# Turning the rows and columns of a segment softmax by block transposes on VectorE, and spreading destination scores by a transfer

## The chip, the cores and the metric

The kernel runs on one core of a Trainium2 chip. The metric is the device time of one execution in microseconds (us). The core has five engines that each work through an instruction queue of their own in order: TensorE (PE in the profile, PEld for its weight loads), VectorE (DVE), ScalarE (ACT), GpSimd (POOL) and SyncE (SP, which only issues transfers here). They meet through semaphores. SBUF is the on-chip memory of 128 partitions, PSUM the smaller memory that TensorE writes its products into.

## What is computed

A graph attention layer over 12,500 nodes of 64 features and 400,000 edges of 64 features, the edges sorted by destination. In the reference, without its helpers:

```python
h_src = nfeats[src]
h_dst = nfeats[dst]
z_att = jnp.concatenate([h_src, h_dst, efeats], axis=-1)
e = jax.nn.leaky_relu(z_att @ W_attn + b_attn, negative_slope=0.01)[:, 0]
m = jnp.concatenate([h_src, efeats], axis=-1) @ W_ne
emax = jax.ops.segment_max(e, dst, num_segments=N)
ex = jnp.exp(e - emax[dst])
denom = jax.ops.segment_sum(ex, dst, num_segments=N)
alpha = ex / denom[dst]
z = jax.ops.segment_sum(alpha[:, None] * m, dst, num_segments=N)
out = jax.nn.relu(jnp.concatenate([nfeats, z], axis=-1) @ W_out)
```

The result is the layer norm of x + out over the features.

## The kernel before

**Tiling.** A group is 512 edges: 128 partitions (p) of 4 consecutive edges (t). There are 782 groups. The first 83 full ones, whose few destinations have very many edges each, are the dense part (the generator `dense_part`, three chunks of 32, 28 and 24 groups). The others are cut into 36 chunks of 20 groups (the last two are shorter), and a chunk into parts of SG = 4 groups, 175 parts in all. The edges of one group have destinations inside a window of S = 48 nodes, so a one-hot of 48 columns against a group's first destination says where an edge goes.

**A chunk.** The loop over chunks does this, in program order:
- `indices` and `slots_of` turn the source and destination numbers of a chunk two ahead into columns (TensorE transposes L155, ScalarE copies).
- For each part, `gather` loads the edge features ze by one SyncE transfer (L181) and the source rows zx by 16 indirect transfers that GpSimd issues (L190). Both come from rings of ZB = 8 buffers. Then `scores` computes the attention scores. It loads wrow, 48 destination scores for each of the 4 groups, as one row on one partition (L202); a TensorE matmul of that row with ones_row (L203) copies it to all 128 partitions, into win. VectorE then runs a chain: L207 (ze times the attention weights w_edge), L209 (sum), L214, L216 (the one-hot, hot), L221 (hot times win), L224 (sum), L225, L226 (leaky relu), about 5.8 us a part. The tile fixed is one PSUM bank that holds slots, w_edge, w_src, alpha and win.
- `softmax` works on the whole chunk. The scores are block transposed (L294), so that a partition holds a row of 128 consecutive edges: partition h*32+g has the h-th quarter of group g. Segments run across the rows, so each of the four running maxima and sums goes in three steps: a scan in each row (L298, L313, L329 and others), a scan over the row results in one line on one partition (L305, L317, L340), and a second scan in each row that starts from the value carried in (L308, L321, L342). `to_row` brings a column of 128 results to one line in the order of the edges: a TensorE matmul with the permuted identity order (L232), read from PSUM. `to_col` brings the line back to a column: VectorE permutes it (L237), TensorE multiplies it by a 1x1 one (L240), VectorE copies the column from PSUM (L242). A softmax has four of each. Three more rows, rw, say where a segment runs on from row to row (L284 to L286 on VectorE, L289 on TensorE, L291 on ScalarE), and fac1, one number that rescales the node shared with the chunk before, is spread to a column in the same manner (L357, L359). ScalarE copies the scores in edge order (e, L296), takes the exponentials (L328, L338) and copies the result to alpha in PSUM (L350).
- `aggregate`, for each part: VectorE makes w = hot times alpha (L365), TensorE 32 float32 matmuls of 64x48 (L373) into a PSUM tile pg, and VectorE adds the four groups of it to acc, the accumulator of all nodes, at an offset read from a register (L383).

A step of `dense_part` is called after each part's scores and after every second part's aggregation, and `finish` writes an output block (layer norm and so on) as soon as its nodes are complete. The dense chunks call the same `softmax`, so there are 39 of these.

**Order.** A scheduler puts all of this into the engines' queues before the run; each engine then works in that order. Which buffer is used is fixed too: sm, the PSUM tile of to_row and to_col, has one buffer, wrow two, pg four, zx and ze eight. A float32 matmul of the program appears in the trace as two weight loads and two multiplications.

Of the kernel before, what the change touches and what calls it, by code (L numbers as in the profile page):

```python
# [23 lines left out]
FLOOR = -1e31  # L24

S = 48
BG = 32
SG = 4
BS = 20
HQ = 4  # L30
# [16 lines left out]
def sorted_path(ctx, tc, x, dst, idx, edge, w_ne, w_attn, b_attn, w_out, out, flag):  # L47
# [10 lines left out]
    nc = tc.nc  # L58
    N, D = x.shape
    E = edge.shape[0]  # L60
    NB = (N + P - 1) // P
# [8 lines left out]
    const = ctx.enter_context(tc.tile_pool(name="const", bufs=1))  # L70
# [3 lines left out]
    ident = const.tile([P, P], F32, name="ident")  # L74
    make_identity(nc, ident)
    ones_row = const.tile([1, P], F32, name="ones_row")
    nc.vector.memset(ones_row, 1.0)
    order = const.tile([P, P], F32, name="order")
    nc.vector.tensor_copy(order.rearrange("k (g h) -> k h g", h=HQ),
                          ident.rearrange("k (h g) -> k h g", h=HQ))  # L80
    attn = const.tile([P, 3 * D], F32, name="attn")
    b_col = const.tile([P, 1], F32, name="b_col")
    wne = const.tile([P, D], F32, name="wne")
    wout = const.tile([D, 2, D], F32, name="wout")
# [20 lines left out]
    wins = [dram.tile([P, S], F32, name=f"wins{k}") for k in range((NG + P - 1) // P)]  # L105
# [8 lines left out]
    tiny = loop.enter_context(tc.tile_pool(name="tiny", bufs=2))  # L114
    psum = loop.enter_context(tc.tile_pool(name="psum", bufs=2, space=bass.MemoryType.PSUM))

    fixed = psum.tile([P, 512], F32, name="fixed", bufs=1)
# [2 lines left out]
    w_edge = fixed[:, S:S + D].unsqueeze(1)  # L120
    w_src = fixed[:, S + D:S + 2 * D].unsqueeze(1)
    alpha = fixed[:, S + 2 * D:S + 2 * D + T * BG].rearrange("p (t g) -> p t g", t=T)
    win = fixed[:, S + 2 * D + T * BG:S + 2 * D + T * BG + SG * S].rearrange("p (g s) -> p g s", g=SG)

    casts = []

# [69 lines left out]
    def scores(g0, n, ze, zx, drel, b0, y, plain):  # L196

        b = g0 - b0
        wrow = tiny.tile([1, SG, S], F32, name="wrow")
        for k in range(g0 // P, (g0 + n - 1) // P + 1):  # L200
            a, b1 = max(g0, k * P), min(g0 + n, (k + 1) * P)
            nc.sync.dma_start(out=wrow[:, a - g0:b1 - g0, :], in_=wins[k][a - k * P:b1 - k * P, :].unsqueeze(0))  # L202
        nc.tensor.matmul(win[:, 0:n, :], ones_row, wrow[:, 0:n, :], start=True, stop=True)  # L203

        yb = y[:, :, b:b + n].rearrange("p t g -> p g t")
        prod = work.tile([P, SG, T, D], F32, name="prod", bufs=1)
        nc.vector.tensor_tensor(prod[:, 0:n], ze[:, 0:n],  # L207
                                w_edge.unsqueeze(1).to_broadcast([P, n, T, D]), op=OP.mult)
        nc.vector.tensor_reduce(yb, prod[:, 0:n], axis=AX.X, op=OP.add)  # L209
        if plain:  # L210
            nc.vector.tensor_tensor(prod[:, 0:n], zx[:, 0:n, :, 0:D],
                                    w_src.unsqueeze(1).to_broadcast([P, n, T, D]), op=OP.mult)
            nc.vector.tensor_reduce(zx[:, 0:n, :, D], prod[:, 0:n], axis=AX.X, op=OP.add)
        nc.vector.tensor_tensor(yb, yb, zx[:, 0:n, :, D], op=OP.add)  # L214
        hot = work.tile([P, SG, T, S], BF16, name="hot", bufs=HB)
        nc.vector.tensor_tensor(  # L216
            hot[:, 0:n], slots.unsqueeze(1).unsqueeze(1).to_broadcast([P, n, T, S]),
            drel[:, :, b:b + n].rearrange("p t g -> p g t").unsqueeze(3).to_broadcast([P, n, T, S]),
            op=OP.is_equal)
        at = work.tile([P, SG, T, D], F32, name="prod", bufs=1)[:, :, :, 0:S]  # L220
        nc.vector.tensor_tensor(at[:, 0:n], hot[:, 0:n],  # L221
                                win[:, 0:n].unsqueeze(2).to_broadcast([P, n, T, S]), op=OP.mult)
        sdst = tiny.tile([P, SG, T], F32, name="sdst")
        nc.vector.tensor_reduce(sdst[:, 0:n], at[:, 0:n], axis=AX.X, op=OP.add)  # L224
        nc.vector.tensor_tensor(sdst[:, 0:n], sdst[:, 0:n], yb, op=OP.add)  # L225
        nc.vector.scalar_tensor_tensor(yb, sdst[:, 0:n], SLOPE, sdst[:, 0:n], op0=OP.mult, op1=OP.max)  # L226
        return hot

    def to_row(col):

        p = psum.tile([P, 3, P], F32, name="sm", bufs=1)[:, 0, :]
        nc.tensor.matmul(p[0:1, :], col, order, start=True, stop=True)  # L232
        return p[0:1, :]

    def to_col(row):
        by_row = tiny.tile([1, P], F32, name="by_row", bufs=1)
        nc.vector.tensor_copy(by_row.rearrange("o (h g) -> o h g", h=HQ),  # L237
                              row.rearrange("o (g h) -> o h g", h=HQ))
        p = psum.tile([P, 3, P], F32, name="sm", bufs=1)[:, 0, :]
        nc.tensor.matmul(p[:, 0:1], by_row, ones_row[:, 0:1], start=True, stop=True)  # L240
        s = tiny.tile([P, 1], F32, name="col")
        nc.vector.tensor_copy(s, p[:, 0:1])  # L242
        return s

    def neighbours(g0, G, name="d3", bufs=2):

# [19 lines left out]
    def softmax(G, y, d3, carry, first, alpha=alpha, tag=""):  # L266
# [3 lines left out]
        far = rows.tile([P, P + 2], F32, name="far3")  # L270
        nc.vector.tensor_scalar(far, d3, FAR, None, op0=OP.mult)

        pf = rows.tile([P, P], F32, name="pf")
# [3 lines left out]
        same = rows.tile([P, P], F32, name="same")  # L277
# [2 lines left out]
        nc.vector.tensor_reduce(up, pf, axis=AX.X, op=OP.max)  # L280
        nc.vector.tensor_tensor(worst[:, 1:2], worst[:, 1:2], up, op=OP.max)

        whole = tiny.tile([P, 3], F32, name="whole")
        nc.vector.tensor_tensor(whole[:, 0:1], far[:, 0:1], far[:, P:P + 1], op=OP.subtract)  # L284
        nc.vector.tensor_tensor(whole[:, 1:2], far[:, 1:2], far[:, P + 1:P + 2], op=OP.subtract)
        nc.vector.tensor_scalar(whole[:, 2:3], whole[:, 0:1], 0.0, None, op0=OP.is_ge)  # L286
        pw = psum.tile([P, 3, P], F32, name="sm", bufs=1)
        for k in range(3):
            nc.tensor.matmul(pw[0:1, k, :], whole[:, k:k + 1], order, start=True, stop=True)  # L289
        rw = tiny.tile([1, 3, P], F32, name="rw", bufs=1)  # L290
        nc.scalar.activation(rw, pw[0:1], AF.Copy)  # L291

        er = rows.tile([P, T, P // T], F32, name="er")
        nc.vector.transpose(er.rearrange("r t q -> r (t q)"), y.rearrange("p t g -> p (t g)"))  # L294
        e = rows.tile([P, P], F32, name="e")
        nc.scalar.activation(e.rearrange("r (q t) -> r q t", t=T), er.rearrange("r t q -> r q t"), AF.Copy)  # L296
        s1 = rows.tile([P, P], F32, name="s1")
        nc.vector.tensor_tensor_scan(s1, pf, e, FLOOR, OP.add, OP.max)  # L298
        ends = to_row(s1[:, P - 1:P])
        top = tiny.tile([1, P + 1], F32, name="top" + tag)  # L300
        if first:
            nc.vector.memset(top[:, 0:1], FLOOR)
# [7 lines left out]
        def total(s, name):  # L310

            b1 = rows.tile([P, P], F32, name="b1")
            nc.vector.tensor_tensor_scan(b1[:, ::-1], pb[:, ::-1], s[:, ::-1], FLOOR, OP.add, OP.max)  # L313
            begins = to_row(b1[:, 0:1])
            rt = tiny.tile([1, P + 1], F32, name=f"rt_{name}", bufs=1)
            nc.vector.memset(rt[:, R:P + 1], FLOOR)
            nc.vector.tensor_tensor_scan(rt[:, 0:R][:, ::-1], rw[:, 1, 0:R][:, ::-1],  # L317
                                         begins[:, 0:R][:, ::-1], FLOOR, OP.add, OP.max)
            bi = to_col(rt[:, 1:P + 1])
            b2 = rows.tile([P, P], F32, name=f"b2_{name}")  # L320
            nc.vector.tensor_tensor_scan(b2[:, ::-1], pb[:, ::-1], s[:, ::-1], bi, OP.add, OP.max)  # L321
            return rt, b2
# [3 lines left out]
        nc.vector.tensor_tensor(dl, e, mx, op=OP.subtract)  # L326
        ex = rows.tile([P, P], F32, name="ex")
        nc.scalar.activation(ex, dl, AF.Exp)  # L328
        nc.vector.tensor_tensor_scan(s1, same, ex, 0.0, OP.mult, OP.add)  # L329
        ends = to_row(s1[:, P - 1:P])  # L330
        den = tiny.tile([1, P + 1], F32, name="den" + tag)
        if first:
            nc.vector.memset(den[:, 0:1], 0.0)
# [18 lines left out]
        if not first:  # L352
            fac1 = tiny.tile([1, 1], F32, name="fac1")
            nc.vector.reciprocal(fac1, rts[:, 0:1])
            nc.vector.tensor_tensor(fac1, fac1, den[:, 0:1], op=OP.mult)
            pfac = psum.tile([P, 3, P], F32, name="sm", bufs=1)[:, 0, :]
            nc.tensor.matmul(pfac[:, 0:1], ones_row, fac1, start=True, stop=True)  # L357
            fac = tiny.tile([P, 1], F32, name="fac" + tag)
            nc.vector.tensor_copy(fac, pfac[:, 0:1])  # L359
        return fac, (top[:, R:R + 1], den[:, R:R + 1])  # L360

    def aggregate(g0, n, ze, zx, hot, b0, fac):
# [32 lines left out]


    prepared = {0: indices(starts[0], sizes[0])}
    nc.sync.dma_start(out=attn, in_=w_attn.rearrange("k o -> o k").to_broadcast([P, 3 * D]))
    CB = 7
    before = ExitStack()  # L400
    pre = before.enter_context(tc.tile_pool(name="pre", bufs=2))
    xts = []
    for c0 in range(0, NB, CB):
        c1 = min(c0 + CB, NB)
# [22 lines left out]
    with before:  # L427
# [14 lines left out]
                in_=xt[:, 0:n, :])  # L442
            nc.vector.tensor_copy(ss[:, c0:c1], xt[:, 0:n, D])
        nc.vector.tensor_scalar(sd, sd, b_col, None, op0=OP.add)
        psd = psum.tile([P, 3, P], F32, name="sm", bufs=1)[0:NB, 0, :]
        nc.tensor.transpose(psd, sd, ident)
        sdt = pre.tile([NB, P], F32, name="sdt", bufs=1)
        casts.append(nc.vector.tensor_copy(sdt, psd).ins)
# [250 lines left out]
    with loop:  # L699
# [54 lines left out]

        bad = tiny.tile([P, 2], F32, name="bad")
        nc.vector.tensor_scalar(bad[:, 0:2], worst[:, 0:2], 0.0, None, op0=OP.is_gt)
        pbad = psum.tile([P, 3, P], F32, name="sm", bufs=1)[0:1, 0:2]
        for k in range(2):
            nc.tensor.matmul(pbad[:, k, :], bad[:, k:k + 1], ident, start=True, stop=True)
        some = tiny.tile([1, 1], F32, name="some")  # L760
# [446 lines left out]
```

## Time and profile before

| | |
|---|---|
| median of 3 runs | 5752.94 us (5750.15 to 5760.51) |
| the profiled execution | 5783.82 us, span 5782.0 us |
| TensorE, multiplying / loading weights | 2351.3 us (41%) / 1647.4 us (28%) |
| VectorE | 2353.6 us (41%) |
| ScalarE | 203.2 us (4%) |
| GpSimd | 2652.0 us (46%) |
| memory traffic | 256.32 MB, mean 44 GB/s |
| mean granted TensorE clock | 0.56 of full speed |

The profile is of one execution, so its durations add up to its own span and not to the median. Its busy times say how long an engine had an instruction in work; they are averages over stages that differ. A line of a view names the engine, the source line, the operation, and what is written and read with partitions x elements. "Idle before, releaser" is the time for which the engine had nothing in work ahead of an instruction, and the instruction that ended most of it; "remote" there is a releaser that the profile does not name, "issue" a time in which the profile shows nothing that the engine waited for.

Costly groups of VectorE, of GpSimd and of the lines concerned:

| line, engine | what | count | busy us | mean ns |
|---|---|---|---|---|
| L190 POOL | gather of 128 source rows | 2716 | 2564.6 | 944 |
| L207 DVE | ze times w_edge | 175 | 212.3 | 1213 |
| L221 DVE | hot times win | 175 | 164.8 | 942 |
| L203 PE | window row to all partitions | 350 | 169.3 | 581 |
| L240 PE | line to column | 312 | 86.9 | 345 |
| L289 PE | three columns to lines | 234 | 56.4 | 409 |
| L232 PE | column to line (two forms) | 312 | 88.9 | 378 to 392 |

### The profile page before, as it was taken

The numbers are of one execution on the slowest core, as the hardware profiler recorded it, in microseconds if no ns is written. First come the engines' busy times: TensorE is split into PE (matmuls) and PEld (weight loads), VectorE is DVE, ScalarE is ACT, GpSimd is POOL, SyncE is SP. The second block draws the span as 40 slices with busy tenths as digits, with TensorE's granted clock in tenths as the row PEclk, the third lists the DMA queues.
The fourth block names the chain that finished last, engine by engine and source line by source line (L and its number), as shares of the span: only waits on it lengthen the run. The fifth ranks groups of instructions, "written<-read, shape, count | busy, mean of one in ns | idle before, by whom it ended". The sixth has DMA issues, their size and how long they took to land.

```text
span 5782.0 us, 47867 instructions
## 1 busy us (share of the span) xinstructions
PE 2351.3 (41%) x16950; PEld 1647.4 (28%) x16950; DVE 2353.6 (41%) x6085; ACT 203.2 (4%) x437; POOL 2652.0 (46%) x2811
## 2 busy tenths in 40 slices
PE   0233333344446333333554544333344544445533
PEld 0122222222324222222232323222232323323323
DVE  4344444333444343334444444134445433353434
ACT  0000000000000000000000000000000000000000
POOL 7444444454443545554444444544443455434441
PEclk9855555555555555555655555555555555555555
DMA  7111111121112112221121212211111212212210
GB/s 123 32 40 39 42 42 39 36 42 36 37 37 58 41 39 45 43 44 33 44 56 37 59 40 47 54 39 40 39 38 36 58 42 47 50 35 55 56 38 15
DMA packets 383261, 256.32 MB, mean 44 GB/s; under 512 B 222971, under 2 KB 337494, under 8 KB 383012
## 3 DMA queue, kind: packets, MB, share of 16 engines
q0 software_dynamic: 89696, 93.36, 10.5%
q1 hardware_dynamic: 266628, 153.14, 10.0%
q10 hardware_dynamic: 26688, 6.67, 0.7%
q8 instruction: 136, 2.23, 0.2%
q14 instruction: 113, 0.93, 0.1%
HBM read 246.27 MB, written 9.07 MB: 44 GB/s over the span
## 4 chain that ended last, share of the span: by engine, by line
issue 27%; PE 25%; DVE 20%; another core or an unknown queue 14%; POOL 9%; DMA 3%; DVEq 1%; ACT 1%; SPq 0%; ACTq 0%; POOLq 0%
PE pg L373 9%; POOL zx L190 9%; PE pg L628 5%; PE pg L653 2%; DVE hot L216 2%; DVE prod L207 2%; PE pg L591 2%; DVE y L209 2%; DVE prod L221 2%; PE fixed L203 1%; PE sm L240 1%; DVE sdst L224 1%; DMA ze_d<-in_x_dram 1%; PE sm L232 1%
## 5 line engine op out<-in xcount | busy, mean ns | idle before, releaser
L190 POOL DMA_INDIRECT zx<-table,srcs x2716 | 2564.6, 944 | 2979.7 <-PE pg L373 1919.1
L373 PE MATMUL pg<-w,ze 128*64 128x48 f32 x5592 | 725.8, 291 | 742.9 <-issue 659.9
L373 PE MATMUL pg<-w,zx 128*64 128x48 f32 x5592 | 732.8, 291 | 659.0 <-issue 637.4
L373 PEld LDWEIGHTS pg<-w,ze 128*64 128x64 f32 x5592 | 622.5, 205 | 850.6 <-issue 748.5
L373 PEld LDWEIGHTS pg<-w,zx 128*64 128x64 f32 x5592 | 628.1, 205 | 708.5 <-issue 676.8
L383 DVE TENSOR_TENSOR acc<-acc,pg 128x48 f32 x699 | 138.7, 198 | 1165.3 <-PE pg L373 573.8
L628 PE MATMUL pg<-hot_c,lot 128*128 128x294 f32 (+2 forms) x672 | 450.8, 808 | 281.7 <-DVE hot_c L626 230.0
L591 PE MATMUL pg<-ss,lot 128*128 128x98 f32 x672 | 170.3, 435 | 611.4 <-DVE lot L588 456.1
L591 PEld LDWEIGHTS pg<-ss,lot 128*128 128x128 f32 x672 | 149.6, 328 | 659.7 <-DVE lot L588 493.4
L365 DVE TENSOR_TENSOR w<-hot,fixed 128x768 f32<-128x768 bf16 x175 | 162.0, 943 | 407.8 <-remote 318.1
L207 DVE TENSOR_TENSOR prod<-ze,fixed 128x1024 f32<-128x1024 f32 x175 | 212.3, 1213 | 269.6 <-PE fixed L203 128.9
L203 PE MATMUL fixed<-wrow,ones_row 1*128 1x192 f32 x350 | 169.3, 581 | 335.5 <-DVE prod L221 153.1
L628 PEld LDWEIGHTS pg<-hot_c,lot 128*128 128x128 f32 x672 | 169.0, 290 | 478.3 <-DVE hot_c L626 289.4
L626 DVE TENSOR_SCALAR hot_c<-fixed,code 128x294 f32<-128x294 f32 (+2 forms) x336 | 203.4, 605 | 192.3 <-remote 120.8
L653 PE MATMUL pg<-sums,ze_d 128*64 128x30 f32 x1568 | 193.6, 292 | 99.1 <-DMA ze_d<-in_x_dram 79.2
L653 PEld LDWEIGHTS pg<-sums,ze_d 128*64 128x64 f32 x1568 | 177.2, 221 | 127.7 <-DMA ze_d<-in_x_dram 89.4
L209 DVE TENSOR_REDUCE y<-prod 128x16 f32<-128x1024 f32 x175 | 211.5, 1209 | 2.4 <-DVE d_d L255 1.2
L588 DVE TENSOR_SCALAR lot<-pg,lane 128x512 f32<-128x512 f32 x84 | 62.6, 745 | 363.6 <-remote 363.5
L203 PEld LDWEIGHTS fixed<-wrow,ones_row 1*128 1x128 f32 x350 | 84.9, 297 | 381.7 <-DVE prod L221 168.0
L224 DVE TENSOR_REDUCE sdst<-prod 128x16 f32<-128x768 f32 x175 | 164.5, 940 | 8.0 <-issue 5.5
L216 DVE TENSOR_TENSOR hot<-fixed,drel 128x768 bf16<-128x768 f32 x175 | 165.5, 946 | 0.0
L221 DVE TENSOR_TENSOR prod<-hot,fixed 128x768 f32<-128x768 bf16 x175 | 164.8, 942 | 0.1
(217 smaller groups left out, 2431.5 us busy)
## 6 DMA issues: line engine op xcount, KB each, us to landing
ze<-in_edge_dram SPq DMA_DIRECT2D x173, 512.0 KB
zx<-table,srcs POOLq DMA_INDIRECT x2716
ze_d<-in_x_dram SPq DMA_DIRECT2D x192, 128.0 KB
ze_d<-in_edge_dram SPq DMA_DIRECT2D x168, 128.0 KB
table<-xt ACTq DMA_DIRECT2D x14, 227.5 KB
xb<-in_x_dram ACTq DMA_DIRECT2D x24, 128.0 KB
out_dram<-sq SPq DMA_DIRECT2D x24, 128.0 KB
xt<-in_x_dram SPq DMA_DIRECT2D x13, 224.0 KB
```

The source lines that it names most:

```text
L190: nc.gpsimd.indirect_dma_start(out=zx[:, g, t, 0:D] if plain else zx[:, g, t, :], out_offset=None, in_=x[:, :] if plain else table[:, :], ...
L203: nc.tensor.matmul(win[:, 0:n, :], ones_row, wrow[:, 0:n, :], start=True, stop=True)
L207: nc.vector.tensor_tensor(prod[:, 0:n], ze[:, 0:n], w_edge.unsqueeze(1).to_broadcast([P, n, T, D]), op=OP.mult)
L209: nc.vector.tensor_reduce(yb, prod[:, 0:n], axis=AX.X, op=OP.add)
L216: nc.vector.tensor_tensor(hot[:, 0:n], slots.unsqueeze(1).unsqueeze(1).to_broadcast([P, n, T, S]), drel[:, :, b:b + n].rearrange("p t g -> ...
L221: nc.vector.tensor_tensor(at[:, 0:n], hot[:, 0:n], win[:, 0:n].unsqueeze(2).to_broadcast([P, n, T, S]), op=OP.mult)
L224: nc.vector.tensor_reduce(sdst[:, 0:n], at[:, 0:n], axis=AX.X, op=OP.add)
L373: nc.tensor.matmul(pg[at:at + D, g, :], z[:, g, t, 0:D], w[:, g, t, :], start=(t == 0), stop=(t == T - 1))
L591: nc.tensor.matmul(ps[:, t, :], lot[:, t, :], ss, start=True, stop=True)
L626: nc.vector.tensor_scalar(hot_c[:, 0:wide * NB], fixed2[:, 0:wide * NB], code[:, t, g:g + 1], None, op0=OP.is_equal)
L628: nc.tensor.matmul(pa[:, 0:wide * NB], lo_w[:, t, :], hot_c[:, 0:wide * NB], start=(t == 0), stop=(t == T - 1))
L653: nc.tensor.matmul(pf[D:P, 0:NA], xb[:, j, :], sums[:, :, c0 + j], start=(c0 + j == 0), stop=(c0 + j == NB - 1))
```

## The change

Three things are replaced.

- `to_row` takes a block of 32 columns instead of a column. VectorE's block transpose turns each 32x32 block of it, so that the wanted column becomes one line on each of the partitions 0, 32, 64 and 96 (tile tr). Four VectorE copies put these four lines of 32 into one line of 128 in edge order. So that the wanted column is the first of its block, two forward scans (into s1) now write reversed.
- `to_col` does the reverse: four copies put a line of 128 into the first column's places of turn (lines on partitions 0, 32, 64 and 96), and a transpose, in the new `turned`, makes the column. rw gets the same with 96 columns (turn3), and fac with fac1 repeated in four copies. The matmuls L232, L240, L289 and L357, ScalarE's copy L291 and the tile order are gone, as are the copies L237 and L242.
- wrow has 128 partitions, and the transfer writes the row to all of them. ScalarE copies it to win, which is a PSUM tile of its own; the matmul L203 is gone.

The PSUM tile sm is gone; win has its place. Two other users of sm, psd and pbad at the start and the end, use pg buffers. The tile attn moves to a pool of the set-up.

```diff
-    win = fixed[:, S + 2 * D + T * BG:S + 2 * D + T * BG + SG * S].rearrange("p (g s) -> p g s", g=SG)
+    win = psum.tile([P, SG, P], F32, name="win", bufs=1)[:, :, 0:S]
...
-        wrow = tiny.tile([1, SG, S], F32, name="wrow")
+        wrow = tiny.tile([P, SG, S], F32, name="wrow")
...
-            nc.sync.dma_start(out=wrow[:, a - g0:b1 - g0, :], in_=wins[k][a - k * P:b1 - k * P, :].unsqueeze(0))
-        nc.tensor.matmul(win[:, 0:n, :], ones_row, wrow[:, 0:n, :], start=True, stop=True)
+            nc.sync.dma_start(out=wrow[:, a - g0:b1 - g0, :],
+                              in_=wins[k][a - k * P:b1 - k * P, :].unsqueeze(0).to_broadcast([P, b1 - a, S]))
+        nc.scalar.activation(win[:, 0:n, :], wrow[:, 0:n, :], AF.Copy)
...
-    def to_row(col):
-
-        p = psum.tile([P, 3, P], F32, name="sm", bufs=1)[:, 0, :]
-        nc.tensor.matmul(p[0:1, :], col, order, start=True, stop=True)
-        return p[0:1, :]
+    def to_row(block):
+
+        tr = rows.tile([P, BG], F32, name="tr")
+        nc.vector.transpose(tr, block)
+        row = tiny.tile([1, P], F32, name="row", bufs=1)
+        for h in range(HQ):
+            nc.vector.tensor_copy(row.rearrange("o (g h) -> o h g", h=HQ)[:, h, :], tr[h * BG:h * BG + 1, :])
+        return row
+
+    def turned():
+        ct = rows.tile([P, BG], F32, name="ct", bufs=2)
+        nc.vector.transpose(ct, turn)
+        return ct[:, 0:1]
 
     def to_col(row):
-        by_row = tiny.tile([1, P], F32, name="by_row", bufs=1)
-        nc.vector.tensor_copy(by_row.rearrange("o (h g) -> o h g", h=HQ),
-                              row.rearrange("o (g h) -> o h g", h=HQ))
-        p = psum.tile([P, 3, P], F32, name="sm", bufs=1)[:, 0, :]
-        nc.tensor.matmul(p[:, 0:1], by_row, ones_row[:, 0:1], start=True, stop=True)
-        s = tiny.tile([P, 1], F32, name="col")
-        nc.vector.tensor_copy(s, p[:, 0:1])
-        return s
+        for h in range(HQ):
+            nc.vector.tensor_copy(turn[h * BG:h * BG + 1, :], row.rearrange("o (g h) -> o h g", h=HQ)[:, h, :])
+        return turned()
...
-        pw = psum.tile([P, 3, P], F32, name="sm", bufs=1)
-        for k in range(3):
-            nc.tensor.matmul(pw[0:1, k, :], whole[:, k:k + 1], order, start=True, stop=True)
+        tr3 = rows.tile([P, 3, BG], F32, name="tr3")
+        nc.vector.transpose(tr3.rearrange("r k g -> r (k g)"), turn3.rearrange("r k g -> r (k g)"))
         rw = tiny.tile([1, 3, P], F32, name="rw", bufs=1)
-        nc.scalar.activation(rw, pw[0:1], AF.Copy)
+        for h in range(HQ):
+            nc.vector.tensor_copy(rw.rearrange("o k (g h) -> o h k g", h=HQ)[:, h], tr3[h * BG:h * BG + 1])
...
-        nc.vector.tensor_tensor_scan(s1, pf, e, FLOOR, OP.add, OP.max)
-        ends = to_row(s1[:, P - 1:P])
+        nc.vector.tensor_tensor_scan(s1[:, ::-1], pf, e, FLOOR, OP.add, OP.max)
+        ends = to_row(s1[:, 0:BG])
...
-            pfac = psum.tile([P, 3, P], F32, name="sm", bufs=1)[:, 0, :]
-            nc.tensor.matmul(pfac[:, 0:1], ones_row, fac1, start=True, stop=True)
+            for h in range(HQ):
+                nc.vector.tensor_copy(turn[h * BG:h * BG + 1, :], fac1.to_broadcast([1, BG]))
             fac = tiny.tile([P, 1], F32, name="fac" + tag)
-            nc.vector.tensor_copy(fac, pfac[:, 0:1])
+            nc.vector.tensor_copy(fac, turned())
```

More of the change, by code (lines that the diff above doesn't have):

```diff
@@ L77, in sorted_path @@
     nc.vector.memset(ones_row, 1.0)
[L78 to L81, printed above, removed]
+    turn = const.tile([P, BG], F32, name="turn")
+    nc.vector.memset(turn, 0.0)
+    turn3 = const.tile([P, 3, BG], F32, name="turn3")
+    nc.vector.memset(turn3, 0.0)
     b_col = const.tile([P, 1], F32, name="b_col")
@@ L281, in softmax @@
         nc.vector.tensor_tensor(worst[:, 1:2], worst[:, 1:2], up, op=OP.max)
[L283 to L286, printed above, removed]
-        pw = psum.tile([P, 3, P], F32, name="sm", bufs=1)
-        for k in range(3):
-            nc.tensor.matmul(pw[0:1, k, :], whole[:, k:k + 1], order, start=True, stop=True)
+        nc.vector.tensor_tensor(turn3[:, 0, 0:1], far[:, 0:1], far[:, P:P + 1], op=OP.subtract)
+        nc.vector.tensor_tensor(turn3[:, 1, 0:1], far[:, 1:2], far[:, P + 1:P + 2], op=OP.subtract)
+        nc.vector.tensor_scalar(turn3[:, 2, 0:1], turn3[:, 0, 0:1], 0.0, None, op0=OP.is_ge)
+        tr3 = rows.tile([P, 3, BG], F32, name="tr3")
+        nc.vector.transpose(tr3.rearrange("r k g -> r (k g)"), turn3.rearrange("r k g -> r (k g)"))
         rw = tiny.tile([1, 3, P], F32, name="rw", bufs=1)
-        nc.scalar.activation(rw, pw[0:1], AF.Copy)
+        for h in range(HQ):
+            nc.vector.tensor_copy(rw.rearrange("o k (g h) -> o h k g", h=HQ)[:, h], tr3[h * BG:h * BG + 1])
         er = rows.tile([P, T, P // T], F32, name="er")
@@ L313, in total @@
             nc.vector.tensor_tensor_scan(b1[:, ::-1], pb[:, ::-1], s[:, ::-1], FLOOR, OP.add, OP.max)
-            begins = to_row(b1[:, 0:1])
+            begins = to_row(b1[:, 0:BG])
             rt = tiny.tile([1, P + 1], F32, name=f"rt_{name}", bufs=1)
@@ L328, in softmax @@
         nc.scalar.activation(ex, dl, AF.Exp)
-        nc.vector.tensor_tensor_scan(s1, same, ex, 0.0, OP.mult, OP.add)
-        ends = to_row(s1[:, P - 1:P])
+        nc.vector.tensor_tensor_scan(s1[:, ::-1], same, ex, 0.0, OP.mult, OP.add)
+        ends = to_row(s1[:, 0:BG])
         den = tiny.tile([1, P + 1], F32, name="den" + tag)
@@ L397, in sorted_path @@
     prepared = {0: indices(starts[0], sizes[0])}
-    nc.sync.dma_start(out=attn, in_=w_attn.rearrange("k o -> o k").to_broadcast([P, 3 * D]))
     CB = 7
@@ L401, in sorted_path @@
     pre = before.enter_context(tc.tile_pool(name="pre", bufs=2))
+    attn = pre.tile([P, 3 * D], F32, name="attn", bufs=1)
+    nc.sync.dma_start(out=attn, in_=w_attn.rearrange("k o -> o k").to_broadcast([P, 3 * D]))
     xts = []
@@ L444, in sorted_path @@
         nc.vector.tensor_scalar(sd, sd, b_col, None, op0=OP.add)
-        psd = psum.tile([P, 3, P], F32, name="sm", bufs=1)[0:NB, 0, :]
+        psd = psum.tile([P, SG, P], F32, name="pg", bufs=4)[0:NB, 0, :]
         nc.tensor.transpose(psd, sd, ident)
@@ L756, in sorted_path @@
         nc.vector.tensor_scalar(bad[:, 0:2], worst[:, 0:2], 0.0, None, op0=OP.is_gt)
-        pbad = psum.tile([P, 3, P], F32, name="sm", bufs=1)[0:1, 0:2]
+        pbad = psum.tile([P, SG, P], F32, name="pg", bufs=4)[0:1, 0:2]
         for k in range(2):
```

## The prediction

> **What bounds the kernel now.** I read the chain of waits on the page first. It has no single owner, so a total over the span can't price the change:
>
> ```profile
> issue 27%; PE 25%; DVE 20%; another core or an unknown queue 14%; POOL 9%; DMA 3%; DVEq 1%; ACT 1%; SPq 0%; ACTq 0%; POOLq 0%
> ```
>
> Next I cut one chunk of 20 groups into stretches (columns: time, length, then busy us and instructions of PE, PEld, DVE, ACT, POOL, then granted clock, DMA share, GB/s):
>
> ```profile
> 2060.00:2084.00 24.00, 4.88 (x73) 4.01 (x71) 2.43 (x7) 0.00 (x0) 16.54 (x18) 0.57 0.32 73
> 2084.00:2107.00 23.00, 6.88 (x66) 6.16 (x68) 5.01 (x12) 0.00 (x0) 13.64 (x15) 0.50 0.15 22
> 2107.00:2128.00 21.00, 10.18 (x44) 7.46 (x41) 19.69 (x40) 0.00 (x0) 15.11 (x16) 0.50 0.28 62
> 2128.00:2165.00 37.00, 14.25 (x54) 8.97 (x54) 30.21 (x89) 2.86 (x8) 0.00 (x0) 0.50 0.05 14
> ```
>
> The kernel alternates. While parts are aggregated (rows one and two) VectorE is busy 2.43 of 24 us and 5.01 of 23, and the part takes as long as its 16 gathers, matmuls and their events. In scores and softmax (rows three and four) VectorE is busy 19.69 of 21 and 30.21 of 37, and in row four GpSimd does nothing. So **in the second phase VectorE's work, and its own waits, count one for one; in the first, work added to VectorE is nearly free.** 36 of the 39 softmaxes are in the second phase, the 3 dense ones inside the first.
>
> The waits that the change touches (engine, name, line, releaser: total us, times, longest):
>
> ```profile
> SPq L202 <- PE fixed L203: 368.4, 105, 31.6
> PE fixed L203 <- DVE prod L221: 153.1, 41, 11.6
> DVE prod L207 <- PE fixed L203: 128.9, 29, 45.6
> DVE prod L207 <- remote: 105.6, 14, 22.1
> DVE col L242 <- PE sm L240: 105.5, 136, 23.3
> ```
>
> SyncE waits longest, but what stands behind its L202 are loads that wait for ring buffers anyway. VectorE's waits are the ones worth money, and one turn of the softmax shows their size:
>
> ```profile
> 2149.15 0.46 DVE L305 TENSOR_TENSOR_SCAN top<-rw,top,sm 1x128 f32<-1x128 f32 x1
> 2149.65 0.26 DVE L237 COPY by_row<-top 1x128 f32<-1x128 f32 x1
> 2149.83 0.13 DVE L304 COPY top<-top 1x1 f32<-1x1 f32 x1
> 2150.58 0.16 DVE L242 COPY col<-sm 128x1 f32<-128x1 f32 x1 [0.61 <-PE sm L240]
> ```
>
> A column costs 0.26 + 0.16 us of copies and 0.61 us of waiting for TensorE's round trip.
>
> **What is removed.** Summed over the trace's VectorE waits below 6 us: L242 82.2 us, L317 29.1, L340 24.8, L305 14.2, L359 6.7, together 157 us over 39 softmaxes, so 145 us for the 36 that count. In scores, L207's small waits for L203 are 57 us (27.4 put down to it, 20.0 "remote", 9.9 "issue"): VectorE's first product waits on the window matmul only because win lies in one PSUM tile with w_edge, and a bank of its own ends that. **−57 us.** L207 also has ten long waits, 187 us, behind a TensorE queue full of L373. What is late next there is the next L383, on the same queue; only the score work that can slip in front (3.5 to 5.8 us each) is gained: **−35 us** (bounds 0 and −187). L203 also leaves TensorE itself (four records for each of 175 matmuls). Much of it, 0.7 to 1.4 us a record beside a gather batch, lies where TensorE is late: **−30** (bounds 0 and −150; near the low end, because the next part is bound by its gather batch of 19.7 us too). The dense softmaxes' long waits on TensorE (23.3, 16.3, 12.5 us) are inside the first phase: **−12** (0 to −52). Together −134 us.
>
> **What is added to VectorE**, for one softmax. Its nearest rows (the last three columns: busy, mean ns | idle before):
>
> ```profile
> L294 DVE STREAM_TRANSPOSE er<-y 128x128 f32<-128x128 f32 x36 | 11.0, 305 | 0.3
> L304 DVE COPY top<-top 1x1 f32<-1x1 f32 x35 | 4.7, 133 | 0.0
> L237 DVE COPY by_row<-top 1x128 f32<-1x128 f32 x36 | 9.2, 256 | 0.7
> ```
>
> A copy of 1x32 lies between the 1x1 (133 ns) and the 1x128 (256): a quarter of the way, 0.165 us. One of 1x96 is about 0.23. A 128x32 block transpose lies between a 128x1 copy (0.157) and the 128x128 (0.305); at the 1 ns per element of these copies, 0.205, and a 128x96 one 0.27. What counts more is how four such copies follow each other, and here **rule and rows must be weighed**. Independent instructions of this trace overlap, dependent ones follow about 0.04 us after the end:
>
> ```profile
> 2166.20 0.15 DVE L284 TENSOR_TENSOR whole<-far 128x1 f32<-128x1 f32 x1
> 2166.27 0.15 DVE L285 TENSOR_TENSOR whole<-far 128x1 f32<-128x1 f32 x1
> ```
>
> Each begins 0.08 us before the former ends, so a copy would cost 0.085. But the Trainium skill ("VectorE: DVE Perf Modes", section "Two Vector instructions with no wait between them") says that an instruction whose first input or output starts in another group of 32 partitions than its predecessor's is held until all earlier ones have finished. The new copies do just that: they read tr at partitions 0, 32, 64, 96, or write turn there. The trace has one such pair, memsets at partitions 32 and 64:
>
> ```profile
> 5443.87 0.06 DVE L168 MEMSET drel<- 32x4 f32 x1
> 5443.97 0.06 DVE L169 MEMSET drel<- 64x4 f32 x1
> ```
>
> The second begins 0.04 us after the first's end although it needs nothing of it. That agrees with the rule, on one pair. By the rule a copy costs 0.165 + 0.04 = 0.205 us:
> - to_row: transpose 0.245 with its gap, four copies 0.82 = 1.065, four times: 4.26.
> - to_col: the same 1.065 less the two removed copies (0.26 + 0.157) = 0.65, four times: 2.59.
> - rw: transpose 0.31, four 1x96 copies at 0.27 = 1.39; it was ScalarE's, and comes to VectorE whole.
> - fac: four copies and a transpose, 1.07; its last copy stays.
>
> 9.31 us, times 36: **+335 us**; less the 145 of waits, +190. With overlapping copies: to_row 0.705, to_col 0.29, rw 1.03, fac 0.705, so 5.7 us, 206 in all, less 145: +61. I take held. The ends: copies at 133 ns and transposes at 0.157 make held +130; copies at 256 ns and transposes at 0.305, +345. So a column, held, costs what the TensorE trip did (1.1 against 1.17 us); the loss is in to_row (the trip was 0.5 to 0.7 us of waiting, none at L305 where other work filled it), rw and fac. The 3 dense softmaxes' 28 us lie beside VectorE's idle time in aggregation: 0; uncovered, +28.
>
> A second rule speaks against the change: by "SBUF — State Buffer", section "A bandwidth-pool intuition that's wrong (but worth ruling out)", a float32 SBUF-to-SBUF copy on VectorE locks GpSimd out while it would write gather descriptors. By the row, GpSimd is busy 0.00 us of the 37 us of scores' end and softmax, so I put 0; by the rule only copies that meet gathers count, those of the dense softmaxes, under 28 us.
>
> **Moved to other queues.** ScalarE takes 175 copies of 128x192 (its 128x128 copy into PSUM took 0.269 us, so about 0.33), 58 us on an engine busy 4%, and loses 39 of rw (0.48). Each waits for L221 of the part before (one bank), and for the spread wrow. L221 now waits for ScalarE; behind L221 on VectorE stand all later scores. Ahead of it stand L207, L209 and L216 of the same part (1.2 + 1.2 + 0.95 us), which cover 0.33. In ScalarE's order the next chunk's first win copy stands ahead of this chunk's e, ex and alpha; its L221 is done by then, so only a late wrow could hold these. The wrow transfer is written to 128 partitions instead of one, 96 KB each; SyncE's 175 issues stay. Some 22,400 more packets at 35 ns, the mean of queue q1 (266628 packets in 10.0% of 16 engines), is 49 us of one engine's time spread over 16; a 128 KB load landed 3.5 us after its issue, and two buffers let wrow start about two parts (12 us) ahead: 0. With no cover, 3.5 us a part. The scans that now run reversed (L298, L329) change by 0.01 us (L298 0.41, the reversed L313 0.42): 0. The removed order tile, attn's pool and the psd and pbad banks are set-up: 0.
>
> **Sum.** +190 − 134 = +56 us. On the profiled execution (span 5782.0, time 5783.82) that gives 5840; it lies 30.9 above the median, and I carry the difference over: 5752.94 + 56 = **5809 us**, 1.0% slower.
>
> **Rivals.**
> 1. *The copies overlap* (0.085 each): +61 − 134 = −73, **5680 us**, faster. For it: L284 and L285. Against: the memset pair. It decides as soon as a held step drops below about 0.165 us.
> 2. *TensorE's relief reaches the aggregate phase*: held copies, but the long waits dissolve (−110) and L203's slots too (−90): 190 − 57 − 12 − 110 − 90 = −79, **5674 us**. For it: TensorE has 25% of the chain. Against: the gathers, 16 at 0.944 us and their gaps, set the step of 23 us by themselves.
> 3. *The spread wrow comes late*, and L221, or e behind win in ScalarE's queue, waits 1 us per part: +175, **5984 us**. Against: 12 us of lead. It decides when the transfer takes more than that.
>
> **Chances.** Forecast 0.60, rival 1 0.18, rival 2 0.14, rival 3 0.08. The forecast's own range: copies at their cheap end with gains of 190 instead of 134 (+130 − 190, 5693) to copies half way to their dear end with gains of 85 (+268 − 85, 5936). Down to 5640 the range takes in rivals 1 and 2 with some 35 us to spare; rival 3 is left out. **5640 to 5935.** A change of 0.2%, 11.5 us, is what can be told from none. Faster: 0.15 + 0.12 of rivals 1 and 2 and 0.03 of the forecast, 0.30; same 0.09; slower 0.61.
>
> **What would show it.** Right: L237's four copies begin 0.19 to 0.22 us apart; no VectorE wait on a softmax row or column; the softmax stretch (16.7 us from L294 to L349 before) some 4 to 5 us longer; L207 without small waits; the aggregate step of 23 us unchanged. Wrong: copies 0.09 apart; aggregate steps shorter by over 1 us; L221 or L298 waiting for ScalarE; gathers longer than 944 ns.

## The result and the profile after

| | median | against the kernel before, same chip |
|---|---|---|
| before | 5752.94 us (5750.15 to 5760.51) | |
| changed | 5788.71 us (5780.48 to 5797.30) | 1.006 (95%: 1.0045 to 1.0075) |

The change costs 36 us, where 56 were forecast. The profiled execution of the changed kernel took 5793.67 us (span 5792.0), so the spans of the two profiles differ by 10 us only, while the medians differ by 36. A single execution shows where time goes, but it doesn't measure a difference of half a per cent.

First the waits of the changed kernel, in the columns of before (L203, L205, L209, L223 are the old L202, L203, L207, L221; L387 is the old L383):

```profile
SPq L203 <- ACT win L205: 447.9, 87, 39.3
ACT win L205 <- DVE prod L223: 3075.7, 128, 105.0
DVE prod L223 <- ACT xtt L523: 4.9, 1, 4.9
DVE acc L387 <- remote: 608.4, 42, 20.2
```

L209 and the columns have no line left: VectorE waits for none of the removed matmuls any more. ScalarE, which now makes win, waits for VectorE and not the other way round, apart from one wait of 4.9 us. Part of the old waits has come back one step later, at the addition that takes in the aggregation's matmuls: L387's "remote" was 463.2 us before (its wait for L377 fell from 573.8 to 555.5).

Next the same turn of a softmax in the changed kernel (start, duration, instruction):

```profile
2174.62 0.21 DVE L234 STREAM_TRANSPOSE tr<-s 128x32 f32<-128x32 f32 x1
2174.87 0.78 DVE L237 COPY row<-tr 1x32 f32<-1x32 f32 x4
2175.68 0.47 DVE L344 TENSOR_TENSOR_SCAN den<-rw,den,row 1x128 f32<-1x128 f32 x1
2176.19 0.75 DVE L247 COPY turn<-den 1x32 f32<-1x32 f32 x4
2176.98 0.21 DVE L242 STREAM_TRANSPOSE ct<-turn 128x32 f32<-128x32 f32 x1
2177.23 0.48 DVE L346 TENSOR_TENSOR_SCAN s<-same,ct,ex 128x128 f32<-128x128 f32 x1
```

Four copies take 0.75 to 0.78 us, 0.19 each, one after the other. From the start of the first transpose to the line's scan it is 1.06 us, from the end of that scan (2176.15) to the next one 1.08. No wait is left, and nearly all the time is copies. The groups of these lines (shape, count | busy us, mean ns | idle before):

```profile
L237 DVE COPY row<-tr 1x32 f32<-1x32 f32 x624 | 115.2, 185 | 12.3 <-issue 2.8
L295 DVE COPY rw<-tr 1x96 f32<-1x96 f32 x156 | 37.0, 237 | 10.3 <-issue 7.1 <-DVE prod L223 0.4
L234 DVE STREAM_TRANSPOSE tr<-b 128x32 f32<-128x32 f32 x78 | 16.0, 206 | 0.1
L209 DVE TENSOR_TENSOR prod<-ze,fixed 128x1024 f32<-128x1024 f32 x174 | 210.5, 1210 | 0.0
```

And a chunk by stretches (columns as before; aggregation, the overlap with the next chunk's first score, scores, softmax):

```profile
2084.00:2115.00 31.00, 5.01 (x39) 4.33 (x40) 2.11 (x4) 0.00 (x0) 23.38 (x26) 0.54 0.23 44
2115.00:2129.00 14.00, 3.09 (x34) 2.49 (x34) 5.81 (x15) 0.33 (x1) 5.35 (x6) 0.50 0.13 31
2129.00:2164.00 35.00, 12.28 (x44) 9.30 (x44) 33.91 (x68) 1.34 (x4) 13.36 (x15) 0.50 0.23 52
2164.00:2185.00 21.00, 1.07 (x8) 0.95 (x8) 18.91 (x88) 2.71 (x7) 0.00 (x0) 0.50 0.05 11
```

VectorE is now busy 33.91 of 35 us in the scores and 18.91 of 21 in the softmax, with GpSimd at 0.00 there: the second phase has become VectorE alone. Over the whole span VectorE's busy time went from 2353.6 to 2616.5 us and TensorE's from 2351.3 to 1926.2. Splitting both executions at each softmax (first to last block transpose) shows where the time went. The sums below are worked out from the traces' timelines, one execution each:

| | span | 36 softmaxes | all the rest |
|---|---|---|---|
| before | 5782.0 | 677 | 5105 |
| changed | 5792.0 | 779 | 5013 |

The softmaxes cost 102 us more, the rest 92 us less. Of the rw transposes and copies, 78 of 195 lie inside the softmaxes; the others are part of "the rest".

### The profile page after: what moved, and what is told of

Read it like the earlier page. It is cut to its first block, busy times and chain, and to the rows that moved or that the text cites. A ratio compares the mean times of both kernels' runs of the same rounds, so it can differ in the third digit from the quotient of the medians.

```text
span 5792.0 us, 47177 instructions
## 1 busy us (share of the span) xinstructions
PE 1926.2 (33%) x15668; PEld 1420.2 (25%) x15668; DVE 2616.5 (45%) x7714; ACT 249.9 (4%) x575; POOL 2651.7 (46%) x2811
## 3 DMA queue, kind: packets, MB, share of 16 engines
q14 instruction: 129, 1.06, 0.1%
## 4 chain that ended last, share of the span: by engine, by line
issue 28%; DVE 26%; another core or an unknown queue 17%; PE 16%; POOL 8%; DMA 3%; DVEq 1%; SPq 1%; ACT 1%; ACTq 0%; POOLq 0%
POOL zx L191 8%; PE pg L377 8%; PE pg L633 4%; DVE prod L223 2%; DVE prod L209 2%; DVE hot L218 2%; DVE sdst L226 2%; DVE row L237 2%; DVE turn L247 2%; DMA ze_d<-in_x_dram 2%; DVE hot_c L631 1%; DVE y L211 1%; PE pg L658 1%; DMA zx<-table,srcs 1%
## 5 line engine op out<-in xcount | busy, mean ns | idle before, releaser
L377 PE MATMUL pg<-w,ze 128*64 128x48 f32 x5592 | 716.4, 291 | 1349.1 <-issue 767.0
L377 PEld LDWEIGHTS pg<-w,ze 128*64 128x64 f32 x5592 | 622.0, 206 | 1426.9 <-issue 1112.1
L377 PE MATMUL pg<-w,zx 128*64 128x48 f32 x5592 | 726.0, 290 | 688.8 <-issue 671.0
L377 PEld LDWEIGHTS pg<-w,zx 128*64 128x64 f32 x5592 | 625.3, 205 | 743.3 <-issue 706.0
L387 DVE TENSOR_TENSOR acc<-acc,pg 128x48 f32 x699 | 137.8, 197 | 1227.8 <-remote 608.4
L205 ACT ACTIVATE win<-wrow 128x192 f32<-128x192 f32 x175 | 58.3, 333 | 3684.4 <-DVE prod L223 3075.7
L209 DVE TENSOR_TENSOR prod<-ze,fixed 128x1024 f32<-128x1024 f32 x175 | 211.5, 1208 | 0.0
L642 DVE TENSOR_TENSOR sums<-sums,pg 128x294 f32 (+2 forms) x84 | 46.4, 553 | 323.0 <-remote 207.6
L605 DVE TENSOR_TENSOR sel<-hot_h,pg 128x392 f32<-128x392 bf16 x84 | 47.1, 561 | 295.4 <-remote 245.8
L223 DVE TENSOR_TENSOR prod<-hot,win 128x768 f32<-128x768 bf16 x175 | 164.9, 942 | 5.1 <-ACT xtt L523 4.9
```

The source lines that it names most:

```text
L209: nc.vector.tensor_tensor(prod[:, 0:n], ze[:, 0:n], w_edge.unsqueeze(1).to_broadcast([P, n, T, D]), op=OP.mult)
L223: nc.vector.tensor_tensor(at[:, 0:n], hot[:, 0:n], win[:, 0:n].unsqueeze(2).to_broadcast([P, n, T, S]), op=OP.mult)
L377: nc.tensor.matmul(pg[at:at + D, g, :], z[:, g, t, 0:D], w[:, g, t, :], start=(t == 0), stop=(t == T - 1))
L387: nc.vector.tensor_tensor(ag, ag, pg[:, g, :], op=OP.add)
```

## The experiments

The kernels ran on several chips, and on some of these the kernel before itself takes some 5750 us, on others some 3600. Each kernel is therefore compared with the kernel before on its own chip, and kernels of different chips only where that one takes the same. No chip is on record for two rounds of runs, so "kind of chip" below names what differed and not its cause.

**The softmax part alone.** It is the changed kernel with the window row as before:

```diff
-    win = psum.tile([P, SG, P], F32, name="win", bufs=1)[:, :, 0:S]
+    win = fixed[:, S + 2 * D + T * BG:S + 2 * D + T * BG + SG * S].rearrange("p (g s) -> p g s", g=SG)
...
-        wrow = tiny.tile([P, SG, S], F32, name="wrow")
+        wrow = tiny.tile([1, SG, S], F32, name="wrow")
...
-        nc.scalar.activation(win[:, 0:n, :], wrow[:, 0:n, :], AF.Copy)
+        nc.tensor.matmul(win[:, 0:n, :], ones_row, wrow[:, 0:n, :], start=True, stop=True)
```

> The softmax part of the change alone (rows, columns, rw and fac by block transposes and copies; the window row still goes to all partitions by the matmul into the shared bank, as before). Theory (the copies are held, and the loss is all here): the softmax grows by 4 us, 36 times, less about 12 us of dense waits: 5870 to 5930 us. Rival (the softmax part is about neutral, the loss comes from the spread transfer or the copy on ScalarE): 5740 to 5790 us.

Measured: 5909.14 us, 1.0265 (1.0235 to 1.0294) of the before's 5754.13, so +155 us, inside the theory's range. The loss is here. Its softmaxes sum to 761 us, and the rest of its span of 5905.9 to 5145, 40 more than before. That is what rw outside the softmaxes should cost: 119 of its 195 instructions lie there; at some 0.27 us a step they are 32 us. L207 (here L208) waits as it did:

```profile
DVE prod L208 <- PE fixed L204: 134.4, 33, 45.4
DVE prod L208 <- remote: 107.0, 16, 19.1
```

Against it, the changed kernel is 120 us faster (5909.14 to 5788.71, each beside a kernel before of 5753 or 5754): that is what the window part brings.

**The window part alone**, with the softmax left on TensorE:

```diff
-    win = fixed[:, S + 2 * D + T * BG:S + 2 * D + T * BG + SG * S].rearrange("p (g s) -> p g s", g=SG)
+    shared = psum.tile([P, 512], F32, name="pp", bufs=1)
+    win = shared[:, 256:256 + SG * S].rearrange("p (g s) -> p g s", g=SG)
...
-        nc.tensor.matmul(win[:, 0:n, :], ones_row, wrow[:, 0:n, :], start=True, stop=True)
+        nc.scalar.activation(win[:, 0:n, :], wrow[:, 0:n, :], AF.Copy)
...
-        pp = psum.tile([P, 2 * T, BG], F32, name="pp", bufs=1)
+        pp = shared[:, 0:256].rearrange("p (c g) -> p c g", c=2 * T)
```

> The window part alone: spread transfer, copy by ScalarE, win in a bank that no product of a score reads (it shares that of the index transposes, pp); softmax through TensorE as before. Theory: the 57 us of L207's small waits go, some 35 of the long ones, some 30 of TensorE's relief: 5610 to 5660 us. Rival (the transfer and ScalarE cost something): 5753 us or more.

Measured: 5699.04 us, 0.9891 (0.9864 to 0.9918). It is faster, but by 55 us and not by 90 or more, outside both expectations. The bank shared with the index transposes has a price in the trace:

```profile
DVE srcs L159 <- PE pp L156: 23.4, 11, 6.1
DVE srcs_d L159 <- remote: 50.5, 2, 38.4
```

VectorE's casts of the indices (srcs and srcs_d), which read that bank, wait 74 us. They waited 3.4 us before, and 3.4 again in the last run of the window part below, where nothing shares the bank.

**Only win's place**, with TensorE's matmul kept (the edit above without the lines of the transfer and the copy).

> Only win's place is changed, as in the window part alone; the row is still spread by TensorE's matmul from one partition. Theory (most of the window gain is that L207 no longer waits for TensorE): 5650 to 5690 us, some 30 us behind the window part alone. Rival (the gain is the relief of TensorE, four records for each of 175 matmuls out of its queue): 5735 to 5755 us.

Measured: 5715.11 us, 0.9917 (0.9888 to 0.9946), 39 us faster. Both expectations missed: it lies between them. The intervals of this run and of the window part alone overlap, so most of that part's gain can be the end of L207's wait; how much TensorE's relief adds was not resolved.

**The window part without the shared bank.** The softmax's TensorE results use pg buffers, so that win has a bank for itself.

```diff
-    win = fixed[:, S + 2 * D + T * BG:S + 2 * D + T * BG + SG * S].rearrange("p (g s) -> p g s", g=SG)
+    win = psum.tile([P, SG, P], F32, name="win", bufs=1)[:, :, 0:S]
...
-        p = psum.tile([P, 3, P], F32, name="sm", bufs=1)[:, 0, :]
+        p = psum.tile([P, SG, P], F32, name="pg", bufs=4)[:, 0, :]
```

> The window part alone once more, with win in a PSUM bank of its own and the softmax's TensorE results in pg buffers instead, so that the index transposes share no bank with win. The two parts alone gave +155 and -55 us, together +36: 65 us are not additive. Theory A (the shared bank spoiled the window run: its casts of indices and a dense softmax waited for TensorE): about 5640 us. Theory B (with the softmax still on TensorE the window part is worth only some 55 us, because TensorE's queue stays in the chain of scores and softmax): 5690 to 5710 us.

> The window part alone without the shared bank, a third time, for a chip on which the kernel before takes some 5750 us. There: Theory A (the shared bank spoiled the first window run, and the parts add up) 0.978 to 0.983; Theory B (with the softmax still on TensorE the window part is worth only 1%) 0.989 to 0.992. On a chip where it takes some 3600 us: 0.999 as before, and the question stays open.

The first of these ran where the kernel before takes 3598.17 us: 3595.02, 0.9991 (0.9983 to 1.0000), which says nothing of A or B; a repetition did no better (0.9990, 0.9983 to 0.9996). The third time the chip was one with a before of 5774.30 us: 5697.52, 0.9872 (0.9854 to 0.9889), 77 us faster, between A and B. Its trace says why it is not more: outside its softmaxes the span is 4974 us, 131 less than in the trace of before, but its softmaxes sum to 708, 31 more. Of these, 28 are idle time of VectorE, most of it ahead of the first scan that reads a row from a pg buffer; that it queues for the buffers there is likely, but was not tested. So the window part is worth some 130 us outside the softmax: 131 here, 132 between the softmax part alone and the changed kernel. Put beside rw's 40, it gives the changed kernel's −92, and the two parts add up there. In the kernels that carry the window part alone, the makeshift for the missing PSUM bank ate part of the gain. This step rests on single executions on different chips.

**The copies from one quadrant.** In the changed kernel, all copies start at partition 0, so none changes the quadrant (a group of 32 partitions); the rows and columns hold the first quarter's values only:

```diff
-            nc.vector.tensor_copy(row.rearrange("o (g h) -> o h g", h=HQ)[:, h, :], tr[h * BG:h * BG + 1, :])
+            nc.vector.tensor_copy(row.rearrange("o (g h) -> o h g", h=HQ)[:, h, :], tr[0:1, :])
...
-            nc.vector.tensor_copy(turn[h * BG:h * BG + 1, :], row.rearrange("o (g h) -> o h g", h=HQ)[:, h, :])
+            nc.vector.tensor_copy(turn[0:1, h * BG:(h + 1) * BG], row.rearrange("o (g h) -> o h g", h=HQ)[:, h, :])
```

> The changed kernel with every one of the four copies of a row, a column, rw or fac starting at partition 0 on both sides (the same count and sizes; rows and columns then hold the first quarter's values only, so the softmax computes with other numbers). Theory (the copies are held because they start in another group of 32 partitions): their step falls from 0.19 to about 0.10 us, 3.4 us a softmax and 0.4 for rw, 36 times: 5640 to 5680 us. Rival (a copy's step is its own length, wherever it starts): step 0.19 us still, 5780 to 5800 us.

Measured: 5610.62 us, 0.9755 (0.9725 to 0.9785). Against the changed kernel's 1.006 that is 3.05%, 175 us. The same turn of a softmax:

```profile
1962.38 0.21 DVE L234 STREAM_TRANSPOSE tr<-s 128x32 f32<-128x32 f32 x1
1962.62 0.44 DVE L237 COPY row<-tr 1x32 f32<-1x32 f32 x4
1963.10 0.47 DVE L344 TENSOR_TENSOR_SCAN den<-rw,den,row 1x128 f32<-1x128 f32 x1
1963.61 0.46 DVE L247 COPY turn<-den 1x32 f32<-1x32 f32 x4
```

As many copies of the same size, but four take 0.44 to 0.46 us in place of 0.75 to 0.78. One copy still lasts some 0.175 us; they now overlap and begin 0.09 us apart. In both kernels the second to fourth copies of to_row and to_col have, with fewer than ten exceptions in 936, no wait of their own. So the step of 0.19 us is a hold, and it alone is worth five times the whole result.

Two things change together in this run: the copies no longer start in another quadrant than the one before, and none goes from one quadrant to another. The memsets on record separate the two. The pair at partitions 32 and 64 that the prediction shows moves nothing between quadrants, and its second begins 0.04 us after the first has ended. Of the 20 other pairs of neighbouring memsets in the trace of before, which start at the first partition of their tiles, 18 overlap: the second begins 0.01 to 0.05 us before the first has ended (the other two begin 0.6 and 2.3 us after it). So the change of the start quadrant seems enough for a hold, on this one pair.

At 5610.62 us the run is 30 us below the theory's range, which counted the copies alone. The 36 softmaxes sum to 622 us against 779, 157 less; some 110 of these lie in the copies. Part of the others lies with instructions that stand beside copies and are held too. From the start of the reciprocal L348 to that of L350, with two copies of fac in between, it is 1.37 us in the changed kernel and 0.97 here, where the copies overlap the reciprocal. The scheduler also puts a few instructions in another order in this kernel, which is not separated.

**The changed kernel with the matmul into a bank of its own**, and **columns by transposes** (to_col as in the change, rows, rw and fac on TensorE, window part as in the run without sharing):

> The changed kernel with the window row spread by TensorE's matmul from one partition again, into a bank of its own; softmax by transposes and copies. Between the softmax part alone (5909) and the changed kernel (5789). Theory A (the decoupling of L207 is most of the window gain, as 39 of 55 us with the old softmax): 5800 to 5830 us. Theory B (with the softmax off TensorE, TensorE's relief is most of it: the score part would still wait in its queue): 5860 to 5900 us.

> As the window part alone without the shared bank, and to_col by four copies and a transpose on VectorE; to_row, rw and fac stay on TensorE. Theory (a held column costs what TensorE's trip did, 1.08 against 1.17 us; the loss of the change is in to_row, rw and fac): within 15 us of the run without it. Rival (columns share the loss in proportion to their copies, 16 of 40): 50 us or more slower than it.

Both ran where the kernel before takes 3598.17 us: 1.0009 (1.0002 to 1.0016) and 0.9988 (0.9982 to 0.9995). Repeated beside the changed kernel itself, on a chip of the same kind (before 3600.67), they gave 1.0008 (0.9999 to 1.0016) and 0.9986 (0.9980 to 0.9993), against 0.9990 without the transposed columns. The expectation of the changed kernel there was:

> The changed kernel itself, beside the next three. Where the kernel before takes some 5750 us: 1.004 to 1.008 of it, as shown. Where it takes some 3600 us, as in the last three runs, and GpSimd's gathers set the pace: 0.998 to 1.004, since added work on VectorE lies beside gathers there.

Measured: 3599.97 us, 0.9997 (0.9989 to 1.0005): no change. Times on these chips can't decide what the first two were made for, because the softmax is hidden there. The lengths of the 36 softmaxes say something on the columns: from first to last transpose the median is 18.66 us with columns through TensorE and 18.29 with columns by copies, but the sums are 698 and 708 (18.55 and 18.45, 699 and 708 in the first pair of runs). The median says shorter, the sum longer, and both differ by 2% at most: a held column costs about what the trip did. How the 120 us of the window part divide between the wait and TensorE's relief stays open.

**Why one kernel takes 5790 or 3600 us.** The changed kernel's groups, first where it takes 5792, then where it takes 3599 (busy us, mean ns | idle before, what ended most of it):

```profile
L191 POOL DMA_INDIRECT zx<-table,srcs x2716 | 2565.5, 945 | 2991.9 <-PE pg L377 1973.4
L377 PEld LDWEIGHTS pg<-w,ze 128*64 128x64 f32 x5592 | 622.0, 206 | 1426.9 <-issue 1112.1
L377 PEld LDWEIGHTS pg<-w,zx 128*64 128x64 f32 x5592 | 625.3, 205 | 743.3 <-issue 706.0
```

```profile
L191 POOL DMA_INDIRECT zx<-table,srcs x2716 | 2581.7, 951 | 842.6 <-issue 787.5
L377 PEld LDWEIGHTS pg<-w,ze 128*64 128x64 f32 x5592 | 440.6, 171 | 717.0 <-issue 365.1
L377 PEld LDWEIGHTS pg<-w,zx 128*64 128x64 f32 x5592 | 441.0, 171 | 8.5 <-issue 6.8
```

And a chunk where it takes 3599 (softmax first, then aggregation, then scores):

```profile
1448.00:1470.00 22.00, 1.06 (x8) 0.95 (x8) 20.03 (x90) 3.99 (x8) 16.51 (x19) 0.50 0.20 36
1470.00:1490.00 20.00, 16.34 (x336) 15.36 (x337) 13.49 (x42) 0.00 (x0) 15.12 (x17) 0.75 0.54 148
1490.00:1510.00 20.00, 5.71 (x29) 3.99 (x25) 19.75 (x40) 0.67 (x2) 15.12 (x17) 0.59 0.34 77
```

A gather costs the same on both. But where the kernel is slow, TensorE's aggregation records hang on nothing that the profile shows (1112 and 706 us against 365 and 7), and the gathers wait 1973 us for buffers that TensorE is late to free: 39 records in 31 us there, against 336 in 20 us here, at a granted clock of 0.54 there and 0.75 here.

The pauses have a pattern. In the stretch 2084 to 2115 us, 25 weight loads of L377 begin within 1.3 us; after that one begins at 2102.40, 2103.80, 2105.90, 2108.00, 2110.10, 2112.20 and 2115.00, at steps of 1.4, 2.1 and 2.8 us. Over the span, 1185 steps from one such load to the next are of 0.4 to 6 us, 1672 us in all, and 70% of them are within 0.03 us of a multiple of 0.7 us, where chance would give 9%. In the trace of 3599 us there are 6 steps of that size.

Where TensorE runs freely, GpSimd gathers through the softmax too (16.51 of 22 us). A chunk takes 100 us, about its 80 gathers at 0.951 us and the 0.29 us between them (99 us), so VectorE's longer softmax lies beside the gathers and costs nothing. What holds TensorE back on the one kind of chip, and whether its clock is cause or consequence, wasn't found.

## Why the prediction was right, step by step

- **Two phases, and VectorE's work counts in the second.** Right for the kind of chip it was made on: the softmax part alone cost 155 us. It is not a property of the kernel alone: where the gathers set the pace the changed kernel took 0.9997 of the kernel before.
- **Copies held on a change of quadrant.** Right, and it decided the sign. The four-copy step was put at 0.82 us and measured 0.75 to 0.78. The single durations were right as well (copies 0.165 and about 0.23 us against 0.185 and 0.237, a 128x32 transpose 0.205 against 0.206). The worth of the hold was not: the sums with and without it, +190 and +61, lie 129 us apart, and the run without it came out 175 us faster, since, for one thing, instructions beside the copies are held too. Rival 1, overlap, falls: the copies don't overlap, and the kernel in which they do ran at 5611, below rival 1's 5680.
- **to_col about even, loss in to_row, rw and fac.** Supported by the softmaxes' lengths (sums of 708 against 698 us), not by a time.
- **The softmax part, +190 − 12 = +178.** Measured +155. That it came so near is in part luck, because two terms were both too large. In the trace of the softmax part alone, VectorE's busy time inside the 36 softmaxes went from 463 to 680 us and its idle time from 214 to 82. So 217 us were added and 132 removed, where about 305 (335 without the three fifths of rw that lie elsewhere) and 145 were forecast. Of the first difference some 18 us are the copies (0.765 us for four instead of 0.82) and some 35 the transposes: they were put at 0.245 us each, and most move VectorE on by 0.12 only, because neighbours overlap them. The rest is open. The changed kernel's softmax grew by 2.8 us on average where 4 to 5 were named.
- **The window part, −57 − 35 − 30 = −122.** Measured −120 between the softmax part alone and the changed kernel. The long waits did turn up again at L387, as forecast, and the step from one part's additions to the next's stayed (medians of the steps under 40 us: 21.9 before, 22.6 after). How the sum divides into its three terms was not shown, so their agreement may be chance.
- **ScalarE and the spread transfer at 0.** Right: 4.9 us of wait in the whole span; rival 3 falls. The 22,400 packets at 35 ns are 49 us on each of the 16 engines, 784 in all, and not 49 in all; it had no effect that shows. **Rival 2** falls too: the gain stayed at the small sums.
- **GpSimd locked out by copies: 0.** Right where GpSimd is idle in the softmax (0.00 busy above). Where gathers run beside the copies, it is the copies that wait (last section).

## What to carry to other kernels

Several small VectorE copies in a row cost their full length each when they start at different groups of 32 partitions (0.19 us here), and half of it when they don't (0.09); replacing a round trip through TensorE by four of them gained nothing here, although every wait disappeared. A value that shared a PSUM bank with the operands of the next instruction made that instruction wait for its writer. The window part, which moves it out of that bank and off TensorE, was the useful part of this change: alone it took 0.9872 of the kernel before where the gathers don't set the pace, and 0.9990, about nothing, where they do. Before pricing work on one engine, find out which engine sets the pace in that stage on the chip in question.

## What was not expected of the hardware

The same program took 5792 us on one chip and 3599 on another, at mean granted clocks of 0.561 and 0.632, with gathers of equal length and VectorE busy for 2616 and 2656 us. Most of the difference shows as TensorE's pauses in the aggregation, on a grid of 0.7 us.

Where GpSimd gathers during the softmax, some of the small copies get longer. The same group of L237 there, and one gather with one copy:

```profile
L237 DVE COPY row<-tr 1x32 f32<-1x32 f32 x624 | 136.2, 218 | 9.6
```

```profile
1453.52 0.94 POOL L191 DMA_INDIRECT zx<-table,srcs  x1 [0.30 <-issue]
1454.04 0.44 DVE L237 COPY row<-tr 1x32 f32<-1x32 f32 x1
```

The mean is 218 ns against 185 with GpSimd idle, but most copies are as short as before. Of the 1248 copies of to_row and to_col, 215 last over 0.25 us, up to 0.45. Every one of them runs beside a gather, and 200 end within 0.03 us of a gather's end, as the one shown does (1454.48 and 1454.46). The 257 copies that meet no gather take 0.181 us on average, and none is long. So a copy that begins in the last 0.45 us of a gather ends only with it. The gathers don't get longer by the copies: their mean is 951 ns in this kernel and in the window part alone on the same chip, which has none of these copies. Which part of a gather holds the copy was not tested.
